# A skip term moved from VectorE into TensorE's sum over states

## The chip, the cores and the metric

The kernel runs on one NeuronCore of a Trainium2 chip. A core has engines that run beside each other, each with its own queue of instructions, which it works through in order: TensorE (PE, matrix products; its weight loads are shown apart as PEld), VectorE (DVE), ScalarE (ACT), GpSimd (POOL) and SyncE (SP, which here only issues DMAs). They wait for each other by semaphores. Data lies in SBUF (128 partitions); TensorE writes its sums to PSUM, which VectorE and ScalarE read.

The metric is the device time of one execution in microseconds (us). The profile is of one execution.

## The reference, cut to what matters

The reference runs four blocks over an image batch of 2 x 128 channels x 64 x 64: a state-space block ("the layers", two layers of Mamba with a feed-forward part), two attention blocks and a multi-scale block. The change touches the first alone. In each of its layers, with 256 inner channels and 16 states per channel:

```
u, z = split(LN(t) @ in_w.T)
u  = silu(causal_conv(u) + conv_b)
dt, B, C = split(u @ xproj_w.T);  dt = softplus(dt @ dt_w.T + dt_b)
h[t] = exp(dt * A) * h[t-1] + dt * u * B          # per channel and state
y  = sum over states of h * C  +  u * ssm_D       # the skip term is u * ssm_D
t  = t + (y * silu(z)) @ out_w.T
t  = t + ffn(LN(t))
```

`ssm_D` is one number per layer and inner channel.

## The kernel before, in words

The layers are cut into 32 items: 2 images x 2 layers x 8 chunks of 512 positions, in this order. An item has 32 slots, one for each scan. Channels and states lie together on the partitions: a group is 32 channels x 4 states (partitions) with 4 more states behind each other, so a group has four scans of 128 x 512, and an item has eight groups. The kernel's order is written out by hand: `slot` issues the recurrent work of a slot and then the entries that `background` has put at it with `at(slot, function, ...)`. Each engine works through its part of that list in order, so an entry's slot sets what it stands behind on its queue.

The recurrent work, by the names used later:

- `spread_dtu` (L406, "pdu"): TensorE spreads dt*u of a group over the states, one matmul of 128 x 128 by 512 columns, in the first slot of the group before (slots 0, 4, 8, ...). Its PSUM pool has one buffer, so it waits until `times_b` of the group before has read it.
- `times_b` (L412): VectorE multiplies it by B, into a tile `h` of 128 x 2048, in the last slot of a group (slots 3, 7, 11, ...). `h` has five buffers.
- `decay` (L419, "da"): ScalarE computes exp(dt*A) for the scan four slots later, into one of four PSUM buffers.
- `scan` (L430): VectorE's recurrence. Behind the fourth scan of a group GpSimd copies the last column (`carry`, L432) and multiplies `h` by C (L433).
- `y_pair` (L445): TensorE sums two groups over their states into one PSUM tile `py`, with 16 rows in the trace, at slots 4, 12, 20 and 28. The tile of a half (128 channels, `j` = 0 or 1) takes two `y_pair`s: slots 12 and 20 for `j` = 0, slots 28 and 4 (of the next item) for `j` = 1. `py` has one buffer.
- `y_out` (L453): VectorE computes u*ssm_D + py and writes it over u, at slot 24 for `j` = 0 and at slot 7 of the next item for `j` = 1.
- `gate` (L456): GpSimd multiplies z by it, at slot 7; `mix_out` ("po", L462) uses the product on TensorE at slot 9.

Beside this run, for the next, the same and the earlier items: convolution taps ("pu", L333, and its copy L339), "pz" (L346 and its copy L349), layer norm ("pc" L267, its square L274 and copy L275, "var" L281, the Newton step "nt" L297 on GpSimd and L298 on ScalarE, "pr" L306), silu (L353, slot 11), "pd" (L362, its copy "dbl" L366), "pt" (L381) and softplus (L387, slot 17), dt*u ("dtu", L393, GpSimd, slot 18), the feed-forward part ("ph", "hid", "pf", L478 to L499). Items 0 to 5 and 14 to 21 also do `embed` for an item two later, items 10 to 17 and from 26 on also `out_mm` for an item two earlier (L504 and L505, at slot 11).

`silu` and `soft_plus` each load a table before and after their work. All the products of layer norm, convolution, feed-forward and projections share two PSUM buffers ("mm").

Of the kernel before, what the change touches and what calls it, by code (L numbers as in the profile page):

```python
# [6 lines left out]
F32 = mybir.dt.float32  # L7
AF = mybir.ActivationFunctionType
ALU = mybir.AluOpType
# [6 lines left out]
P = 128  # L16
CH = 512
# [5 lines left out]
NJ = DI // P  # L23
# [44 lines left out]
def tile_conv_seq(ctx: ExitStack, tc, x, consts, vecs, wemb, wlay, wconv, wdt, wqkv, wsmall, wms, out):  # L68
    nc = tc.nc
# [22 lines left out]
    def load_x(b, c):  # L92
        nc.sync.dma_start(xv(b, c), x[b, :, c * RPC : (c + 1) * RPC, :])
# [6 lines left out]
    ident = kc[:, K_ID : K_ID + P]  # L100
# [3 lines left out]
    def v1(name, i=0):  # L104
        return vec[:, VEC[name] + i : VEC[name] + i + 1]
# [10 lines left out]
    with tc.manual_schedule(), ExitStack() as s:  # L116
        wp = layers.enter_context(tc.tile_pool(name="l0w", bufs=1))
        spl = layers.enter_context(tc.tile_pool(name="l0t", bufs=1))
        mm = layers.enter_context(tc.tile_pool(name="l0mm", bufs=2, space=PSUM))
        yp = layers.enter_context(tc.tile_pool(name="l0y", bufs=1, space=PSUM))  # L120
# [11 lines left out]
        sel = wp.tile([P, 32], F32, name="sel")  # L132
# [9 lines left out]

        nc.scalar.preload_act_table_set(EXP_LN_SET)
        load_x(0, 0)
        wl, wu, wd, am, cws = [], [], [], [], []

        def load_layer(l):
            cw = sp.tile([P, KC + 1, DI], F32, name="cw", tag="h", bufs=5)
# [86 lines left out]
        items = [(b, l, c) for b in range(B) for l in range(NL) for c in range(NCH)]  # L235
        NI, NST, NSL = len(items), 8, 32
        st = [{} for _ in items]
# [3 lines left out]
        def has(i):  # L241
            return 0 <= i < NI

        def vl(name, i, k=0):
            return v1(f"{name}{items[i][1]}", k)
# [189 lines left out]
        def y_pair(g):  # L435

            i, s_ = divmod(g, NST)
            j, gg = divmod(s_, 4)
            if gg == 0:
                st[i]["py", j] = yp.tile([P, CH], F32, name="py", tag="y")  # L440
            py = st[i]["py", j]
            for m in range(4):
                for k in range(2):
                    r = 32 * (gg + k)
                    nc.tensor.matmul(  # L445
                        py[r : r + 32, :], lhsT=sel, rhs=st[i]["h", s_ + k][:, m, :], start=(m == 0), stop=(m == 3),
                        tile_position=(0, r),
                    )


        def y_out(i, j):
            u = st[i]["u"][:, j, :]
            nc.vector.scalar_tensor_tensor(u, u, vl("ssm_D", i, j), st[i].pop(("py", j)), ALU.mult, ALU.add)  # L453

        def gate(i):
            nc.gpsimd.tensor_tensor(st[i]["z"], st[i]["z"], st[i]["u"], ALU.mult)  # L456
# [55 lines left out]
        def background(i):  # L512

            todo = [[] for _ in range(NSL)]

            def at(t, f, *a):
                todo[t].append((f, a))

            n, p, q, r = i + 1, i - 1, i - 2, i + 2
            if has(q):  # L520
                at(3, gelu, q)
                at(6, ffn_down, q, (0, 1)), at(7, ffn_down, q, (2, 3)), at(9, ffn_add, q)
                at(11, out_mm, q), at(12, out_add, q)
            if has(p):
                at(7, y_out, p, 1), at(7, gate, p)
                at(9, mix_out, p), at(11, mix_add, p)
            if has(n):
                at(0, pu_taps, n, 0, (0, 1)), at(1, pu_taps, n, 0, (2, 3)), at(2, pu_out, n, 0)
                at(3, pu_taps, n, 1, (0, 1)), at(4, pu_taps, n, 1, (2, 3)), at(5, pu_out, n, 1)
                at(13, xproj, n), at(14, xproj_out, n), at(14, spread_bc, n, 0), at(22, spread_bc, n, 1)  # L530
                at(15, dtproj, n, 0), at(16, dtproj, n, 1), at(17, soft_plus, n), at(18, dt_end, n)
            if has(i):
                at(1, pz_mm, i, 0), at(3, pz_out, i, 0)
                at(5, pz_mm, i, 1), at(6, pz_out, i, 1)
            if has(i) or has(n):
                at(11, silu, i, n)
            if i == -1:
                at(1, load_rest), at(7, prepare, 1), at(9, through_out)
                for k in range(3):
                    at(8 + k, fold, k), at(23, fold_out, k)  # L540
                at(19, spread_dtu, 0), at(26, times_b, 0)
            pair = [(k, second) for k, second in ((p, True), (r, False)) if has(k)]
            if has(r):
                at(10, embed, r), at(11, embed_out, r)
            w, m = {}, len(pair)
            for k, (it, second) in enumerate(pair):
                at(12 + 2 * k, ln_centre, w, k, it)
                at(13 + 2 * k, ln_square, w, k, it)
                at(27, ln_spread, w, k, m), at(28, ln_scale, w, k, it)
                at(29, ln_shift, w, k, it, second)  # L550
            if pair:
                at(17, ln_var, w, m), at(18, ln_eps, w, m), at(19, ln_rs, w, m), at(20, ln_newton, w, m), at(21, ln_step, w, m)
            if has(p):
                for f in range(4):
                    at(30 + f // 2, ffn_up, p, f)
            if has(i):
                at(24, y_out, i, 0)
            return todo
# [6 lines left out]
        def slot(i, todo, t_):  # L565
            t = i * NSL + t_
            g, m = divmod(t, 4)
            if m == 0 and 0 <= g + 3 < NG:
                spread_dt(g + 3)
            if m == 0 and 1 <= g + 1 < NG:  # L570
                spread_dtu(g + 1)
            if m == 0 and g % 2 == 1 and 0 <= g - 3 < NG:
                y_pair(g - 3)
            if 0 <= t < NT:
                scan(t)
            if 0 <= t + 4 < NT:
                decay(t + 4)
            if m == 3 and 1 <= g + 1 < NG:
                times_b(g + 1)
            for f, a in todo[t_]:  # L580
                f(*a)
        for i in range(-2, NI):
            todo = background(i)
            for t_ in range(NSL):
                slot(i, todo, t_)
        todo = background(NI)
        for t_ in range(8):
            slot(NI, todo, t_)
# [313 lines left out]
        for k in range(8, 2 * NSL):  # L902
            if k == NSL:
                todo = background(NI + 1)
            for _ in range(int(beside[k - 8]) if k - 8 < len(beside) else 0):
                next(steps, None)
            slot(NI + k // NSL, todo, k % NSL)
# [7 lines left out]
        for now in range(NALL + LAG + 8):  # L915
            r, u = divmod(now, NU)
# [65 lines left out]
    with ExitStack() as s, tc.manual_schedule():  # L982
# [59 lines left out]
        items = [(b, c) for b in range(B) for c in range(NCH)]  # L1042
        NI = len(items)
        st = [{} for _ in items]
# [433 lines left out]
```

## Time and profile before

| | |
|---|---|
| Median of 3 runs | 4975.6 us (4974.84 to 4981.31) |
| Profiled execution | 4975.69 us, span 4973.9 us |
| Layers (the part changed) | from the start to about 2102 us of the span |
| Busy over the span | PE 93%, DVE 80%, ACT 47%, POOL 47% |
| Busy in 490 to 1010 us (some eight items) | DVE 484.8, PE 474.0, ACT 381.9, POOL 371.6 of 520 us |
| VectorE's `y_out` (L453) | 64 times, 46.8 us in all, 732 ns each |
| `y_pair` on TensorE (L445) | 2048 rows, 513.6 us |

How to read it: a line of the timeline has the start in us from the start of the span, the time in us, the engine, the line of the kernel, the operation, what it writes and reads, the shapes and how many instructions are merged (x6); in brackets at the end stands how long the engine was idle before it and what ended that wait. A group has count, busy us, mean ns of one, then the idle time of the engine in front of it. A wait for several semaphores is put down to the one that came last. Matmuls are pipelined and their ends are modelled, so rows can overlap by a tenth of a microsecond or several. The granted TensorE clock is 1 at full speed.

### The profile page before, as it was taken

The numbers are of one execution on the slowest core, as the hardware profiler recorded it, in microseconds if no ns is written. First come the engines' busy times: TensorE is split into PE (matmuls) and PEld (weight loads), VectorE is DVE, ScalarE is ACT, GpSimd is POOL, SyncE is SP. The second block draws the span as 40 slices with busy tenths as digits, with TensorE's granted clock in tenths as the row PEclk, the third lists the DMA queues.
The fourth block names the chain that finished last, engine by engine and source line by source line (L and its number), as shares of the span: only waits on it lengthen the run. The fifth ranks groups of instructions, "written<-read, shape, count | busy, mean of one in ns | idle before, by whom it ended". The sixth has DMA issues, their size and how long they took to land.

```text
span 4973.9 us, 48435 instructions
## 1 busy us (share of the span) xinstructions
PE 4643.1 (93%) x14634; PEld 2218.0 (45%) x14634; DVE 3975.5 (80%) x4155; ACT 2361.8 (47%) x3225; POOL 2331.1 (47%) x1974
## 2 busy tenths in 40 slices
PE   6899999999988899899999999999999999999997
PEld 2222222222222222266667766666666666333332
DVE  6999999999999999878886677767766775667775
ACT  4677777777777777632222232233333332323332
POOL 3777776676777777613332233333333332334231
PEclk8888898988999989899999999999999999999998
DMA  6333332223333333214444444444444443000000
GB/s 163 68 67 68 69 69 67 67 67 71 69 69 69 71 73 71 69 36 126 113 111 123 113 109 115 122 99 111 114 101 98 114 112 83 3 7 7 7 5 9
DMA packets 242485, 386.28 MB, mean 78 GB/s; under 512 B 88608, under 2 KB 89136, under 8 KB 233776
## 3 DMA queue, kind: packets, MB, share of 16 engines
q1 hardware_dynamic: 193072, 316.01, 26.1%
q10 hardware_dynamic: 49152, 67.17, 5.4%
q8 instruction: 117, 1.92, 0.2%
q14 instruction: 144, 1.18, 0.1%
HBM read 101.09 MB, written 13.37 MB: 23 GB/s over the span
## 4 chain that ended last, share of the span: by engine, by line
PE 46%; POOL 25%; issue 12%; DVE 8%; DMA 4%; SPq 3%; ACT 3%; ACTq 0%; POOLq 0%; DVEq 0%
POOL h L433 19%; PE pq L780 13%; PE po L830 13%; DVE tr L810 3%; SPq L821 3%; DMA pt<-tr 3%; PE pa L677 2%; PE pf L1135 2%; PE pqkv L1162 2%; PE pw L1221 1%; POOL dtu L393 1%; POOL z L456 1%; PE pb L677 1%; PE pfus L1286 1%; PE psc L1186 1%
## 5 line engine op out<-in xcount | busy, mean ns | idle before, releaser
L817 POOL COPY pt<-tr 32x512 f32<-32x512 f32 x1024 | 644.7, 630 | 1410.8 <-DVE tr L810 700.7
L430 DVE TENSOR_TENSOR_SCAN h<-da,carry,h 128x512 f32<-128x512 f32 x1024 | 1241.6, 1265 | 65.1 <-ACT da L419 36.2
L433 POOL TENSOR_TENSOR h<-h,cb 128x2048 f32<-128x2048 f32 x256 | 1160.9, 4535 | 20.8
L780 PE MATMUL pq<-k,q 128*128 128x512 f32 x2048 | 963.4, 593 | 12.5 <-DVE sc L785 12.5
L830 PE MATMUL po<-pt,vt 128*128 128x256 f32 x4096 | 965.6, 379 | 3.5 <-POOL pt L817 3.5
L795 ACT ACTIVATE sc<-sc,nm 128x2048 f32<-128x2048 f32 x256 | 510.5, 1995 | 886.8 <-DVE nm L791 656.4
L830 PEld LDWEIGHTS po<-pt,vt 128*128 128x128 f32 x4096 | 777.9, 190 | 309.5 <-issue 227.5
L785 DVE TENSOR_SCALAR_CACHE_REDUCE sc<-pq 128x1024 f32<-128x1024 f32 x512 | 624.8, 1222 | 333.8 <-PE pq L780 311.7
L419 ACT ACTIVATE da<-dtb,am 128x512 f32<-128x512 f32 x1024 | 681.4, 684 | 221.3 <-DVE h L430 205.6
L412 DVE TENSOR_TENSOR h<-bb,pdu 128x2048 f32<-128x2048 f32 x256 | 581.4, 2271 | 85.4 <-PE py L445 28.3
L810 DVE STREAM_TRANSPOSE tr<-sc 128x2048 f32<-128x2048 f32 x256 | 591.6, 2311 | 65.7 <-DMA pt<-tr 59.3
L445 PE MATMUL py<-h,sel 128*32 128x512 f32 x2048 | 513.6, 645 | 1.8 <-POOL h L433 1.8
L780 PEld LDWEIGHTS pq<-k,q 128*128 128x128 f32 x2048 | 382.2, 190 | 291.5 <-issue 247.4
L406 PE MATMUL pdu<-dtu,fsel 128*128 128x512 f32 x512 | 327.8, 727 | 99.5 <-DVE h L412 97.5
L445 PEld LDWEIGHTS py<-h,sel 128*32 128x32 f32 x2048 | 115.6, 118 | 418.7 <-issue 413.1
L333 PE MATMUL pu<-xn,wu 128*128 128x512 f32 x512 | 245.9, 614 | 10.0 <-ACT u L339 8.3
L406 PEld LDWEIGHTS pdu<-dtu,fsel 128*128 128x128 f32 x512 | 96.6, 215 | 307.4 <-DVE h L412 180.5
L432 POOL COPY carry<-h 128x4 f32<-128x4 f32 x256 | 47.8, 187 | 390.3 <-DVE h L430 386.2
L1228 DVE TENSOR_TENSOR ov<-v,pw 128x2048 f32<-128x2048 f32 x64 | 146.2, 2284 | 65.1 <-PE pw L1221 65.1
L1162 PE MATMUL pqkv<-f,ws 128*128 128x512 f32 x384 | 188.8, 617 | 3.0 <-DVE prod L1179 2.3
L1232 POOL TENSOR_TENSOR ov<-ov 128x2048 f32<-128x2048 f32 x16 | 72.6, 4536 | 237.0 <-DVE ov L1228 237.0
L393 POOL TENSOR_TENSOR dtu<-dt,u 128x1024 f32<-128x1024 f32 x32 | 75.1, 2348 | 199.1 <-ACT dt L387 199.1
(265 smaller groups left out, 5152.4 us busy)
## 6 DMA issues: line engine op xcount, KB each, us to landing
pt<-tr SPq DMA_DIRECT2D x2048, 64.0 KB, 2.0
dtb<-dt SPq DMA_DIRECT2D x1024, 64.0 KB, 2.0
pt<-tr ACTq DMA_DIRECT2D x1024, 64.0 KB, 2.1
bb<-dr SPq DMA_DIRECT2D x128, 256.0 KB, 4.5
cb<-dr SPq DMA_DIRECT2D x128, 256.0 KB, 4.6
uw<-ufold SPq DMA_DIRECT2D x12, 576.0 KB, 4.4
uw<-dkept SPq DMA_DIRECT2D x20, 288.0 KB, 3.1
xt<-in_x SPq DMA_DIRECT2D x16, 256.0 KB, 4.8
```

The source lines that it names most:

```text
L406: nc.tensor.matmul(pdu, lhsT=four(s_ % 4), rhs=st[i]["dtu"][:, s_ // 4, :], start=True, stop=True)
L412: nc.vector.tensor_tensor(h, st[i]["bc", 0], pdu.unsqueeze(1).to_broadcast([P, 4, CH]), ALU.mult)
L419: nc.scalar.activation(da, st[i]["dtb", s_], AF.Exp, scale=am[items[i][1]][:, j, gg, m : m + 1])
L430: nc.vector.tensor_tensor_scan(h[:, m, :], da, h[:, m, :], carries[b, l][:, j, gg, m : m + 1], ALU.mult, ALU.add)
L433: nc.gpsimd.tensor_tensor(h, h, st[i]["bc", 1], ALU.mult)
L445: nc.tensor.matmul(py[r : r + 32, :], lhsT=sel, rhs=st[i]["h", s_ + k][:, m, :], start=(m == 0), stop=(m == 3), tile_position=(0, r),)
L780: nc.tensor.matmul(pq[:, i, :], lhsT=sta["q", r, grp][:, it * P : (it + 1) * P], rhs=sta["k"][:, at : at + CH], start=True, stop=True)
L785: nc.vector.tensor_scalar(dst, pq, 1.0, None, ALU.mult, ALU.max, accum_out=sta["mx"][:, c2 : c2 + 1])
L795: nc.scalar.activation(sc, sc, AF.Exp, bias=nm, scale=scale, accum_out=sm[:, hh : hh + 1])
L810: nc.vector.transpose(tr, sta.pop(("sc", r, blk, hh)).rearrange("p (t r f) -> p r t f", r=NB, f=32))
L817: nc.gpsimd.tensor_copy(dst, src)
L830: nc.tensor.matmul(sta["po", r, grp], lhsT=sta["vt"][:, jt, :], rhs=rhs, start=(jt == 0), stop=(jt == N // P - 1))
```

## The change

The term u*ssm_D is no longer added by VectorE. For each layer of each image GpSimd makes two diagonal matrices of 128 x 128 with ssm_D on the diagonal (`turn_skip`, at slot 2 of the first item of that layer, four times in all). The first `y_pair` of a half opens the sum in `py` with one matmul of the diagonal and u, 128 x 128 by 512 columns; the products over the states add to it. `y_out` becomes a copy of `py` to u on ScalarE, at the same slots as before.

```diff
             if gg == 0:
-                st[i]["py", j] = yp.tile([P, CH], F32, name="py", tag="y")
+                py = st[i]["py", j] = yp.tile([P, CH], F32, name="py", tag="y")
+                nc.tensor.matmul(py, lhsT=skip["now"][:, j, :], rhs=st[i]["u"][:, j, :], start=True, stop=False)
             py = st[i]["py", j]
             for m in range(4):
                 for k in range(2):
                     r = 32 * (gg + k)
                     nc.tensor.matmul(
-                        py[r : r + 32, :], lhsT=sel, rhs=st[i]["h", s_ + k][:, m, :], start=(m == 0), stop=(m == 3),
+                        py[r : r + 32, :], lhsT=sel, rhs=st[i]["h", s_ + k][:, m, :], start=False, stop=(m == 3),
                         tile_position=(0, r),
                     )
...
+        def turn_skip(i):
+            if items[i][2] == 0:
+                dg = skip["now"] = wp.tile([P, NJ, P], F32, name="skip", tag="skip")
+                for j in range(NJ):
+                    nc.gpsimd.tensor_tensor(dg[:, j, :], ident, vl("ssm_D", i, j).to_broadcast([P, P]), ALU.mult)
+
         def y_out(i, j):
-            u = st[i]["u"][:, j, :]
-            nc.vector.scalar_tensor_tensor(u, u, vl("ssm_D", i, j), st[i].pop(("py", j)), ALU.mult, ALU.add)
+            nc.scalar.copy(st[i]["u"][:, j, :], st[i].pop(("py", j)))
...
+            if has(i):
+                at(2, turn_skip, i)
```

More of the change, by code (lines that the diff above doesn't have):

```diff
@@ L144, in tile_conv_seq @@
         load_x(0, 0)
-        wl, wu, wd, am, cws = [], [], [], [], []
+        wl, wu, wd, am, cws, skip = [], [], [], [], [], {}
         def load_layer(l):
```

## The prediction

> **What bounds the kernel now.** The change lies in the layer stage, from the start to about 2102 us of the profiled span of 4973.9 us. I read busy time by stretches first, then the groups of instructions kept apart by shape, then the timeline of one item, engine by engine. A slot is one scan, an item is 32 slots, and a number behind a name here is the slot in its item.
>
> Busy time by stretches: length, then busy us of PE, PEld, DVE, ACT, POOL, then the granted TensorE clock.
>
> ```profile
> core 0: us, PE busy (x) PEld busy (x) DVE busy (x) ACT busy (x) POOL busy (x), PEclk, DMA share, GB/s
> 490.00:1010.00 520.00, 473.96 (x1201) 143.34 (x1199) 484.79 (x362) 381.88 (x541) 371.64 (x178) 0.89 0.32 73
> 628.70:630.70 2.00, 1.96 (x2) 0.50 (x2) 1.91 (x3) 0.59 (x1) 2.00 (x1) 0.50 0.44 101
> 635.40:662.00 26.60, 26.60 (x70) 10.13 (x68) 24.62 (x18) 18.74 (x26) 19.43 (x8) 1.00 0.14 31
> ```
>
> On average VectorE (93%) is a little fuller than TensorE (91%). The last row says more: for 26.6 us TensorE has no gap while VectorE has 2 us of them. The two take turns.
>
> Groups of the layer stage by shape (count, busy us, mean ns):
>
> ```profile
> L453 DVE SCALAR_TENSOR_TENSOR u<-u,vec,py 128x512 f32<-128x512 f32 x64 | 46.8, 732 | 8.6 <-PE py L445 8.6
> L406 PE MATMUL pdu<-dtu,fsel 128*128 128x512 f32 x512 | 327.8, 727 | 99.5 <-DVE h L412 97.5 <-POOL dtu L393 1.8
> L445 PE MATMUL py<-h,sel 128*32 128x512 f32 x2048 | 513.6, 645 | 1.8 <-POOL h L433 1.8
> ```
>
> The first is what goes. The second has the shape of the new product (128x128 weights, 512 columns; two rows for one matmul of the program).
>
> The timeline of items 8 and 9, in which the two removed VectorE instructions stand at 622.25 (slot 24 of item 8) and 653.11 (slot 7 of item 9). First VectorE; in brackets the idle time before, and what ended it:
>
> ```profile
> 622.25 0.72 DVE L453 SCALAR_TENSOR_TENSOR u<-u,vec,py 128x512 f32<-128x512 f32 x1
> 622.88 3.63 DVE L430 TENSOR_TENSOR_SCAN h<-da,carry,h 128x512 f32<-128x512 f32 x3
> ...
> 650.90 2.29 DVE L412 TENSOR_TENSOR h<-bb,pdu 128x2048 f32<-128x2048 f32 x1 [1.01 <-PE py L445]
> 653.11 0.74 DVE L453 SCALAR_TENSOR_TENSOR u<-u,vec,py 128x512 f32<-128x512 f32 x1
> ...
> 659.02 2.29 DVE L412 TENSOR_TENSOR h<-bb,pdu 128x2048 f32<-128x2048 f32 x1 [0.45 <-PE pdu L406]
> ...
> 679.85 1.28 DVE L430 TENSOR_TENSOR_SCAN h<-da,carry,h 128x512 f32<-128x512 f32 x1 [0.63 <-ACT da L419]
> ```
>
> VectorE waits for TensorE at 650.90 and 659.02, that is, on both sides of the second removed instruction. TensorE in the same time:
>
> ```profile
> 628.74 2.07 PE L406 MATMUL pdu<-dtu,fsel 128*128 128x512 f32 x2 [3.10 <-DVE h L412]
> ...
> 657.89 1.02 PE L406 MATMUL pdu<-dtu,fsel 128*128 128x512 f32 x2
> ...
> 661.36 1.12 PE L406 MATMUL pdu<-dtu,fsel 128*128 128x512 f32 x2
> 662.42 3.63 PE L445 MATMUL py<-h,sel 128*32 128x512 f32 x16
> ...
> 669.09 1.13 PE L267 MATMUL pc<-xt,kc 128*128 128x512 f32 x2
> ```
>
> At 628.74 (pdu of slot 28) TensorE has waited 3.10 us for times_b 27 on VectorE. From there to the third matmul behind 669.09 it has no idle mark. The new products stand in just this stretch: slot 28 between 628.74 and the y_pair at 630.74, slot 12 between 661.36 and 662.42. Last, ScalarE and GpSimd:
>
> ```profile
> 622.18 3.88 ACT L419 ACTIVATE da<-dtb,am 128x512 f32<-128x512 f32 x6
> ...
> 661.52 0.59 ACT L466 COPY xt<-po 128x512 f32<-128x512 f32 x1 [1.55 <-PE po L463]
> ...
> 667.98 0.57 ACT L274 ACTIVATE sq<-pc 128x512 f32<-128x512 f32 x1
> ...
> 669.55 0.58 ACT L366 COPY dbl<-pd 40x512 f32<-40x512 f32 x1
> 670.64 0.58 ACT L274 ACTIVATE sq<-pc 128x512 f32<-128x512 f32 x1
> ```
> ```profile
> 613.19 2.35 POOL L393 TENSOR_TENSOR dtu<-dt,u 128x1024 f32<-128x1024 f32 x1 [4.54 <-ACT dt L387]
> ...
> 620.25 1.26 POOL L297 TENSOR_TENSOR nt<-nt,ve 2x512 f32<-2x512 f32 x1
> ```
>
> So an item is one loop: times_b 27 releases pdu 28; TensorE runs on to po at slot 11; ScalarE waits for po, then does silu and softplus; from softplus come the decays of slots 23 and 25, for which VectorE waits; then times_b 27 again. It takes 62.36 us between the dtu of items 8 and 9, and 63.3 on average (110.08 to 2009.27 over 30 items).
>
> **What goes, part by part.** *Slot 7, VectorE.* 0.66 us from the start of the removed instruction to the next scan (653.77). The four scans are then done earlier, and times_b 11 waits for pdu 8 instead: 0.45 becomes 1.11. Bounds of the gain 0 and 0.66; I take 0, because this wait of 0.42 to 0.46 stands at the same place in 29 items (218.61 to 1992.69).
>
> *Slot 24, VectorE.* 0.63 us (622.25 to 622.88). Scan 25 also needs the first of the six decays at 622.18, six in 3.88, so it is there at 622.83. That decay is behind ScalarE's wait for nt, which comes from the softplus by dtu, h and nt on GpSimd. Gain 0.05 here. In items with more TensorE work (out_mm, items 10 to 17 and 26 on) the scan behind the removed instruction already waits (0.88 at 748.16, 0.90 at 1004.13): gain 0. Bounds 0 and 0.63; I take 0, since what is late next is shown in the row.
>
> **What comes.** *The product on TensorE.* Matmuls of that shape follow each other by 0.86 us at full clock (pdu at 657.89, po at 658.75). Where nothing is prefetched it is 1.06 (661.36 to 662.42). In slot 12 it has no wait; in slot 28 it waits for ScalarE's copy of slot 24, some 5 us earlier. I take 0.86; 1.06 is an upper end.
>
> Slot 28 is in the loop's TensorE part, with nothing to hide it: times_b 31 waits already (0.69 at 635.60; put down to a carry that ended at 635.17, but it needs the h buffer that the y_pair reads until 635.51). There the clock is 0.50, and pdu to y_pair takes 2.00 us. If the product lasts twice as long, 1.72; if full clock comes at the same moment as before (between 632.4 and 635.4), work is only moved behind that moment and the delay is 0.86. I take 0.86: with the same instructions half clock goes on for 5.3 us behind the pdu of 1010.0 in item 14, but for some 4.3 behind this one (0.89 on average from 632.4 to 635.4), so a number of matmuls does not end it. 31 of 32 items (the last has TensorE idle there, 3.26 before its ph): 31 x 0.86 = 26.7.
>
> Slot 12 splits. In items 10 to 17 and 26 to 30 TensorE limits what follows: times_b 19 waits for pdu 16 (0.48 at 799.58) or ScalarE waits for pd (0.17 at 796.34). 13 x 0.86 = 11.2; in a few of them ScalarE is the later by a few tenths, which I leave in. In the 18 items 0 to 9 and 18 to 25 ScalarE is late itself: pc of 669.09 ends at 670.22, its square starts at 670.64, so 0.42 is free, and 0.86 - 0.42 = 0.44 goes on to softplus and decay 23, where VectorE waits already (0.63 at 679.85). 18 x 0.44 = 7.9. Bounds per item 0 and 1.06.
>
> *The copies on ScalarE.* 64 of 0.59 us (the z copy of L349 has this shape: 587 ns). Behind slot 24's copy stand decays that wait for scans anyway (0.48 at 626.54, 2.87 at 630.11), so it is covered. Slot 7's copy comes behind decay 11 (654.43 to 655.1) and ends at 655.7; gate, on GpSimd, starts there instead of 654.72 and ends at 658.05, before po at 658.75. ScalarE's next wait, 1.15 for pf at 658.09, takes it up. Cost 0; without that 0.7 of cover, up to 0.6 an item, 18 in all.
>
> *The diagonals.* Four times two GpSimd products of 128x128 at slot 2. By L433 (4535 ns for 2048 columns) about 0.3 each, by L432 (187 ns for 4) at least 0.19: about 2.3 us in all, in front of GpSimd's idle time before the carry of slot 3 (1.5 to 3.7). Cost 0; at most 3. No DMA, no other queue and no table load is touched.
>
> Sum: 26.7 + 11.2 + 7.9 = 45.8. Profiled execution: 4975.69, span 4973.9 and 1.8 around it; the median of the runs is 4975.6. Forecast 4975.6 + 45.8 = 5021.
>
> **Two rules against the rows.** Row: TensorE without idle for the stretches above, VectorE waiting for it. The Trainium skill, Perfetto Trace Analysis, section Identifying the Most-Contended Engine, says that TensorE's busy share is no good measure, that its weight-load share is one, and that the engine with the highest occupancy comes first. By that TensorE stands at 28% (143.34 of 520) and VectorE at 93%, which speaks against my forecast: by the rule the sum would be 46.8 us less, about 4929. I go by the waits.
>
> The Trainium skill, TensorE: Matmul & The Clock Gate, Part 1, has the warm-up as a time of about 3.4 us in a free-running window, not a number of matmuls. By it slot 28 costs 0.86; by twice the time at half clock 1.72, 26.7 more in the sum.
>
> **Rivals.** *VectorE is the bound* (ends on the other side). For it: 93% busy, no wait from 659.02 to 679.85. Against: the waits around both removed instructions. It decides where TensorE is done before VectorE asks, that is, if the waits of 0.45 and 1.01 are not TensorE's. Price at most 64 x 0.73 = 46.8: 4929; with slot 24 alone, 32 x 0.63 = 20, 4955. Chance 0.10.
>
> *Hidden anyway.* Slot 12 covered whole, slot 24's 0.63 real: 26.7 - 20 = 7, 4982. Against: scan 25's decay. Chance 0.04 for within 0.2%, some 10 us, which is about what the measurement tells from no change.
>
> *More than the sum.* Slot 28 at 1.72 and slot 12 at 0.86 throughout: 31 x 2.58 = 80, 5056; for it the half clock at 628.70. Chance 0.16 for over 5040. That the change does not do what it says is excluded by the order of instructions: 64 products and 64 copies stand in it.
>
> **The numbers.** My forecast has 0.70, its own range 5002 (slot 12 free: 26.7) to 5041 (62 x 1.06 = 66). The range of 8 in 10 takes in most of both neighbours: 4988 to 5056. Faster 0.10, same 0.04, slower 0.86.
>
> **What would show it.** Right: times_b 11's wait for pdu grows to about 1.1 or more; the scan behind slot 24 waits for its decay, about 0.6, where it had none; items of about 64 to 66 us; VectorE's busy time down by 47, its idle time up by more. Wrong: dtu to dtu shorter than 62 us in items 2 to 9, or TensorE with idle marks between slots 28 and 12.

## The result and the profile after

The changed kernel takes 5016.99 us (median of 4 runs, 5015.78 to 5020.21), the kernel before beside it 4977.26 us (4974.84 to 4981.31). The ratio is 1.008, with a 95% interval from 1.0063 to 1.0097: slower by 31 to 48 us, where the forecast was 45.8. The profiled execution took 5016.59 us, its span 5014.8.

Of the 40.9 us between the two spans, 34.6 are there at the end of the layers: the first score product of the attention (a row of the tile pq) starts at 2229.3 instead of 2194.7. The other 6.3 come in the stages behind, which the change doesn't touch. These took between 2779.1 and 2786.2 us in the fourteen profiles of this study, one of each kernel, with the same instructions. The runs of the kernel before alone lie between 4974.8 and 4982.2 us, so with one profile each this part can't be told from scatter. Where a few microseconds matter, the layers are compared below; there too each number comes from one profile.

Busy time of the changed kernel in the stretch that was shown for before (length, then PE, PEld, DVE, ACT, POOL, granted clock):

```profile
core 0: us, PE busy (x) PEld busy (x) DVE busy (x) ACT busy (x) POOL busy (x), PEclk, DMA share, GB/s
490.00:1010.00 520.00, 469.95 (x1213) 147.71 (x1212) 468.13 (x340) 384.01 (x550) 360.56 (x172) 0.92 0.31 70
```

VectorE had 484.79 us here before and has 468.13 now. TensorE has more to do for each item and yet is not busier, since the items take longer and its clock is 0.92 instead of 0.89.

The new groups, and two that wait for the sum (count, busy us, mean ns, idle in front and its end):

```profile
L441 PE MATMUL py<-u,skip 128*128 128x512 f32 x128 | 91.5, 807 | 0.5 <-ACT u L459 0.5
L459 ACT COPY u<-py 128x512 f32<-128x512 f32 x64 | 37.2, 582 | 4.4 <-PE py L446 4.4
L462 POOL TENSOR_TENSOR z<-z,u 128x1024 f32<-128x1024 f32 x32 | 75.2, 2350 | 31.1 <-ACT u L459 31.1
L446 PE MATMUL py<-h,sel 128*32 128x512 f32 x2048 | 481.1, 612 | 3.3 <-POOL h L433 3.3
```

The gate on GpSimd now waits 31.1 us for the copy, one microsecond an item: the wait that the forecast had put under cover. The products (the first row) wait 0.5 us in all, for ScalarE's copies, so what they add to TensorE's queue is their own length and not a wait.

The timeline of items 8 and 9 of the changed kernel, VectorE first. These are the scans behind the place of the removed instruction of slot 24, then times_b 7 and times_b 11 around that of slot 7:

```profile
631.51 3.63 DVE L430 TENSOR_TENSOR_SCAN h<-da,carry,h 128x512 f32<-128x512 f32 x3 [1.57 <-ACT da L419]
...
661.22 2.29 DVE L412 TENSOR_TENSOR h<-bb,pdu 128x2048 f32<-128x2048 f32 x1 [1.01 <-PE py L446]
...
669.34 2.29 DVE L412 TENSOR_TENSOR h<-bb,pdu 128x2048 f32<-128x2048 f32 x1 [0.92 <-PE pdu L406]
```

Scan 25 waits 1.57 us for its decay where it had not waited. times_b 11 waits 0.92 for pdu 8 instead of 0.45. From times_b 7 to times_b 11 it is 8.12 us (661.22 to 669.34), and it was 8.12 before (650.90 to 659.02, in the prediction's lines): VectorE's instruction is gone from this stretch, and nothing has become shorter.

TensorE from slot 28 to slot 12 in the same items:

```profile
637.37 2.07 PE L406 MATMUL pdu<-dtu,fsel 128*128 128x512 f32 x2 [2.14 <-DVE h L412]
639.24 1.91 PE L441 MATMUL py<-u,skip 128*128 128x512 f32 x2
641.08 4.75 PE L446 MATMUL py<-h,sel 128*32 128x512 f32 x16
...
668.21 1.02 PE L406 MATMUL pdu<-dtu,fsel 128*128 128x512 f32 x2
...
671.68 1.13 PE L406 MATMUL pdu<-dtu,fsel 128*128 128x512 f32 x2
672.64 1.02 PE L441 MATMUL py<-u,skip 128*128 128x512 f32 x2
673.59 3.63 PE L446 MATMUL py<-h,sel 128*32 128x512 f32 x16
```

The products stand where they were expected, in a queue without idle marks. In slot 12 the product moves the y_pair by 0.95 us (672.64 to 673.59). In slot 28 it moves it by 1.84 (639.24 to 641.08), at half clock. From pdu 28 to pdu 8 it is 30.84 us here, and 29.15 for these items before.

### The profile page after: what moved, and what is told of

Read it like the earlier page. It is cut to its first block, busy times and chain, and to the rows that moved or that the text cites. A ratio compares the mean times of both kernels' runs of the same rounds, so it can differ in the third digit from the quotient of the medians.

```text
span 5014.8 us, 48669 instructions
## 1 busy us (share of the span) xinstructions
PE 4672.2 (93%) x14762; PEld 2247.3 (45%) x14762; DVE 3944.6 (79%) x4091; ACT 2388.8 (48%) x3289; POOL 2332.5 (47%) x1982
## 4 chain that ended last, share of the span: by engine, by line
PE 57%; DVE 12%; POOL 10%; issue 6%; DMA 6%; ACT 5%; SPq 4%; ACTq 0%; DVEq 0%; POOLq 0%
PE pq L788 12%; PE po L838 11%; POOL h L433 7%; PE py L446 5%; PE pu L333 4%; DVE tr L818 4%; DMA pt<-tr 4%; SPq L829 3%; PE pdu L406 2%; PE pa L685 2%; PE ph L484 2%; PE pf L1143 2%; ACT da L419 2%; PE pqkv L1170 2%; DVE h L412 2%
## 5 line engine op out<-in xcount | busy, mean ns | idle before, releaser
L446 PE MATMUL py<-h,sel 128*32 128x512 f32 x2048 | 481.1, 612 | 3.3 <-POOL h L433 3.3
```

The source lines that it names most:

```text
L446: nc.tensor.matmul(py[r : r + 32, :], lhsT=sel, rhs=st[i]["h", s_ + k][:, m, :], start=False, stop=(m == 3), tile_position=(0, r),)
```

## The experiments

The theory is that of the forecast: TensorE's queue from slot 28 to slot 12 sets the time of an item, the products lengthen it, and what leaves VectorE or comes to ScalarE is covered by waits. With it goes a second part, which the changed profile suggests: TensorE's granted clock, which is 0.5 or 1 and nothing else in this trace, gives some of the loss back. The rivals are that VectorE is the bound, and that ScalarE's copies (with the gate's wait) make the loss.

Four numbers are taken from the profile of each kernel. *Item* is the mean from one dtu to the next, over the 30 items from item 1 on. *Stretch* is the mean from the start of pdu 28 to the start of pdu 8 of the next item, over 29 items (from item 2's slot 28 on); slot 28's product lies in it, slot 12's behind it. *Half* is the mean time at clock 0.5 within that stretch. *At full clock* is the stretch less half of that. The kernel before, run again beside each group of these kernels, took 4976.6 to 4977.4 us, so the kernels are compared with each other directly.

| kernel | median us | ratio to before (95%) | item | stretch | half | at full clock |
|---|---|---|---|---|---|---|
| before | 4977 | 1 | 63.31 | 29.38 | 4.97 | 26.90 |
| changed | 5017.0 | 1.0080 (1.0063 to 1.0097) | 64.37 | 29.93 | 4.35 | 27.75 |
| copies on ScalarE, no product | 4981.8 | 1.0008 (0.9999 to 1.0017) | 63.27 | 29.37 | 4.95 | 26.90 |
| products, copies on VectorE | 5020.0 | 1.0086 (1.0071 to 1.0101) | 64.59 | 30.15 | 4.76 | 27.77 |
| slot 28 alone | 5009.0 | 1.0061 (1.0044 to 1.0078) | 64.23 | 30.30 | 5.04 | 27.78 |
| slot 12 alone | 4993.7 | 1.0035 (1.0022 to 1.0048) | 63.75 | 29.35 | 4.91 | 26.89 |
| each product twice | 5074.5 | 1.0192 (1.0177 to 1.0208) | 66.17 | 30.86 | 4.47 | 28.63 |
| products moved | 4971.4 | 0.9990 (0.9980 to 0.9999) | 63.07 | 29.12 | 4.29 | 26.97 |
| moved, slot 27's three times | 4957.5 | 0.9954 (0.9939 to 0.9968) | 62.48 | 27.35 | 0.13 | 27.28 |
| before, one filler | 4962.7 | 0.9970 (0.9958 to 0.9981) | 62.74 | 28.71 | 3.35 | 27.03 |
| before, two fillers | 4950.6 | 0.9947 (0.9930 to 0.9963) | 62.39 | 28.05 | 1.69 | 27.20 |
| before, three fillers | 4964.9 | 0.9974 (0.9965 to 0.9983) | 62.82 | 27.19 | 0.33 | 27.02 |
| half of the change at slot 27 | 4954.0 | 0.9952 (0.9936 to 0.9969) | 62.50 | 27.87 | 1.58 | 27.08 |
| changed, two fillers | 4993.8 | 1.0032 (1.0020 to 1.0044) | 63.73 | 28.47 | 1.18 | 27.88 |

### Copies on ScalarE, no product

```diff
-                nc.tensor.matmul(py, lhsT=skip["now"][:, j, :], rhs=st[i]["u"][:, j, :], start=True, stop=False)
...
-                        py[r : r + 32, :], lhsT=sel, rhs=st[i]["h", s_ + k][:, m, :], start=False, stop=(m == 3),
+                        py[r : r + 32, :], lhsT=sel, rhs=st[i]["h", s_ + k][:, m, :], start=(m == 0), stop=(m == 3),
```

> The copies on ScalarE stay and the skip term is left out: no product on TensorE and no instruction of VectorE for it. TensorE theory: VectorE's 46.8 us were covered by waits and the copies are covered too, so the time is that of before within 10 us (4967 to 4987). VectorE theory (it is the bound, its 47 us are worth their time): 20 to 47 us less than before (4930 to 4957). ScalarE theory (the copies and the gate's wait for them make the loss): 30 to 40 us more (5007 to 5017).

4981.79 us (ratio 1.0008, 0.9999 to 1.0017), and 63.27 us an item against 63.31. VectorE's instruction is gone, 64 copies have come to ScalarE, and the time is that of before. Both rivals fall: freeing VectorE gains nothing, and the copies cost little, 4.4 us by the medians and 1.7 at the end of the layers (2196.4). VectorE's two main groups show where the time went, in the layers before and then in this kernel:

```profile
L430 DVE TENSOR_TENSOR_SCAN h<-da,carry,h 128x512 f32<-128x512 f32 x1024 | 1241.6, 1265 | 65.1 <-ACT da L419 36.2 <-POOL carry L428 3.6 <-ACT hid L479 1.5
L412 DVE TENSOR_TENSOR h<-bb,pdu 128x2048 f32<-128x2048 f32 x256 | 581.4, 2271 | 85.4 <-PE py L445 28.3 <-PE pdu L406 22.3 <-issue 14.7
...
L430 DVE TENSOR_TENSOR_SCAN h<-da,carry,h 128x512 f32<-128x512 f32 x1024 | 1241.5, 1266 | 87.4 <-ACT da L419 54.6 <-POOL carry L428 3.6 <-ACT hid L484 1.5
L412 DVE TENSOR_TENSOR h<-bb,pdu 128x2048 f32<-128x2048 f32 x256 | 581.5, 2272 | 100.0 <-PE pdu L406 37.0 <-PE py L445 28.3 <-issue 15.5
```

The idle time has grown by 22.3 us in front of the scans (65.1 to 87.4), mostly for decays, and by 14.6 in front of times_b (85.4 to 100.0), all for pdu (22.3 to 37.0). These are the two waits that the forecast named for slot 24 and slot 7.

Since the copies came to ScalarE as VectorE's instructions went, the time alone would also fit a gain and a loss that cancel. The rows speak against it. In slot 7 the wait is for TensorE's pdu. In slot 24 of item 8 scan 25 waits for a decay that stands in front of the copy in ScalarE's queue, so the copy doesn't delay it:

```profile
623.97 3.63 DVE L430 TENSOR_TENSOR_SCAN h<-da,carry,h 128x512 f32<-128x512 f32 x3 [0.55 <-ACT da L419]
...
623.27 2.50 ACT L419 ACTIVATE da<-dtb,am 128x512 f32<-128x512 f32 x4
625.72 0.57 ACT L458 COPY u<-py 128x512 f32<-128x512 f32 x1
```

### Products, copies on VectorE

```diff
-            nc.scalar.copy(st[i]["u"][:, j, :], st[i].pop(("py", j)))
+            nc.vector.tensor_copy(st[i]["u"][:, j, :], st[i].pop(("py", j)))
```

> The products stay, the copies of the sums go back to VectorE. TensorE theory: the loss is the products', so the time is that of the changed kernel within 10 us (5007 to 5027). VectorE theory: the copies cost there what they freed, 35 to 47 us above the changed kernel (5052 to 5064). ScalarE theory: the loss goes away, about the time of before (4970 to 4990).

5020.0 us: 3 above the changed kernel. 43.2 us of work have come to VectorE (64 copies of 675 ns), and little of it is seen in the time. At the end of the layers it is 7.9 us (2237.2 against 2229.3), but the stretch at full clock is the same, 27.77 against 27.75: it holds 4.76 us at half clock instead of 4.35, and half of the 0.41, over 31 items, is 6.4. So the loss is the products'.

### Slot 28 alone, slot 12 alone

```diff
             if gg == 0:
                 py = st[i]["py", j] = yp.tile([P, CH], F32, name="py", tag="y")
-                nc.tensor.matmul(py, lhsT=skip["now"][:, j, :], rhs=st[i]["u"][:, j, :], start=True, stop=False)
+                if j == 1:        # slot 28 alone; j == 0 for slot 12 alone
+                    nc.tensor.matmul(py, lhsT=skip["now"][:, j, :], rhs=st[i]["u"][:, j, :], start=True, stop=False)
...
         def y_out(i, j):
-            nc.scalar.copy(st[i]["u"][:, j, :], st[i].pop(("py", j)))
+            if j == 1:
+                nc.scalar.copy(st[i]["u"][:, j, :], st[i].pop(("py", j)))
+                return
+            u = st[i]["u"][:, j, :]
+            nc.vector.scalar_tensor_tensor(u, u, vl("ssm_D", i, j), st[i].pop(("py", j)), ALU.mult, ALU.add)
```

> Only the second half of the channels has the change: product at slot 28, copy on ScalarE at slot 7; the first half is as before. TensorE theory: slot 28's term, 26.7 us at 0.86 each, less what a shorter time at half clock gives back: 12 to 27 us above before (4989 to 5004). VectorE and ScalarE theories see half of the copies: half of the loss, 15 to 22 us.

> Only the first half has the change: product at slot 12, copy on ScalarE at slot 24; the second half is as before. TensorE theory: slot 12's term, 19.1 us by the forecast's sum, less what the clock gives back: 5 to 19 us above before (4982 to 4996), and items 10 to 17 lose more than items 2 to 9. A theory in which nothing but the clock matters: no loss.

Slot 28 alone: 5008.95 us, 31.6 above before, a few microseconds above what was expected; at the end of the layers it is 28.2 (first score product at 2222.9 against 2194.7). The stretch is 0.92 longer and 0.88 at full clock, and the rest of the item (item less stretch) is the same, 33.93.

Slot 12 alone: 4993.68 us, 16.3 above before, and 16.0 at the end of the layers (2210.7). Here the stretch is the same, 29.35 against 29.38, and the rest of the item is 0.47 longer. Items 2 to 9 are longer by 0.32 on average (63.18 against 62.86) and items 10 to 17 by 0.62 (64.815 against 64.196), the order that was expected.

The two parts make 44.2 us in the layers when each stands alone, and 34.6 together. The 9.6 that are missing lie in the stretch: with both it is 27.75 at full clock, as with slot 28 alone (27.78), but the time at half clock is 4.35 instead of 4.97. Half of the 0.62, over 31 items, is 9.6. The two products do not bring this by themselves: with the same two and the copies on VectorE it is 4.76, and the layers take 42.5 us more than before.

### Each product twice

```diff
-                nc.tensor.matmul(py, lhsT=skip["now"][:, j, :], rhs=st[i]["u"][:, j, :], start=True, stop=False)
+                for t in range(2):
+                    nc.tensor.matmul(py, lhsT=skip["now"][:, j, :], rhs=st[i]["u"][:, j, :], start=(t == 0), stop=False)
...
                 for j in range(NJ):
                     nc.gpsimd.tensor_tensor(dg[:, j, :], ident, vl("ssm_D", i, j).to_broadcast([P, P]), ALU.mult)
+                    nc.gpsimd.tensor_tensor(dg[:, j, :], dg[:, j, :], half.to_broadcast([P, P]), ALU.mult)
```

> The changed kernel with each product split into two with half the diagonal: twice the work of TensorE in slots 12 and 28. TensorE theory: another 0.86 at slot 28 and 0.5 to 0.9 at slot 12 in each item, 35 to 55 us above the changed kernel (5052 to 5072). If the loss is not the products': within 10 us of the changed kernel.

5074.51 us, 57.5 above the changed kernel, 2 us over the upper end that was expected. In the stretch one more product is worth 0.88 at full clock again (28.63 less 27.75). The second pair of products costs more than the first, since this time the half clock gives nothing back (4.47 us against 4.35), and the slack of slot 12 is used up: the rest of the item is 35.31 against 34.44.

### Products moved into TensorE's gaps

```diff
             if gg == 0:
-                py = st[i]["py", j] = yp.tile([P, CH], F32, name="py", tag="y")
-                nc.tensor.matmul(py, lhsT=skip["now"][:, j, :], rhs=st[i]["u"][:, j, :], start=True, stop=False)
+                if j == 0:
+                    st[i]["py", j] = yp.tile([P, CH], F32, name="py", tag="y")
...
-                        py[r : r + 32, :], lhsT=sel, rhs=st[i]["h", s_ + k][:, m, :], start=False, stop=(m == 3),
+                        py[r : r + 32, :], lhsT=sel, rhs=st[i]["h", s_ + k][:, m, :], start=(j == 0 and m == 0), stop=(j == 1 and m == 3),
...
+            if gg == 2 and j == 0:
+                product(i, j, False)      # behind the y_pair of slot 20: closes the sum
...
+        def open_second(i):               # at(27, open_second, i), behind ln_spread
+            st[i]["py", 1] = yp.tile([P, CH], F32, name="py", tag="y")
+            product(i, 1, True)
```

> The change with its two products elsewhere: the first half's closes the sum behind the y_pair of slot 20 (not opens it), the second half's opens the sum at slot 27, behind the products of the layer norm. In both places TensorE has idle time before (3.10 us in front of 628.74, 1.54 in front of 623.66). TensorE theory: nearly the whole loss goes, 4965 to 4985, and half clock per item falls, since TensorE idles less. If what costs is any additional product wherever it stands: 5010 to 5020.

4971.42 us (ratio 0.9990, 0.9980 to 0.9999): the loss is gone, with the same 64 products and copies. Half clock falls from 12.88 us an item before to 9.94. TensorE around slot 27, where the timeline of before has 3.10 us without work (the third row, pdu 28):

```profile
619.58 1.98 PE L306 MATMUL pr<-rs,kc 2*128 2x512 f32 x4 [1.08 <-POOL rs L302]
621.48 1.63 PE L455 MATMUL py<-u,skip 128*128 128x512 f32 x2
624.66 2.08 PE L406 MATMUL pdu<-dtu,fsel 128*128 128x512 f32 x2 [1.54 <-DVE h L412]
```

The product fits into the gap, and 1.54 us of it are left: pdu 28 still waits for VectorE and not for the product. Part of the result is a gain by the clock: the stretch has 4.29 us at half clock instead of 4.97. But without it, too, little is lost: at full clock the stretch is 26.97 against 26.90 before, and the rest of the item 33.95 against 33.93, which makes 0.09 an item, some 3 us.

### Filling the gap, to see the clock by itself

In the first of these kernels the moved opening product is issued three times, of which the first two are overwritten:

```diff
-            product(i, 1, True)
+            for k in range(3):
+                nc.tensor.matmul(st[i]["py", 1], lhsT=skip["now"][:, 1, :], rhs=st[i]["u"][:, 1, :], start=True, stop=(k < 2))
```

> As the moved products, with the opening product of slot 27 issued three times (the first two are overwritten), so that TensorE has less idle time in front of slot 28. Clock theory: half clock per item falls by 2 to 4 us against the moved products and the time by 10 to 50 us. Queue theory: the products hold up pdu 28, and the time is 10 to 50 us above the moved ones.

4957.5 us, 14 below the moved products. Half clock per item falls by 3.2 us to 6.73, and from 4.29 to 0.13 us in the stretch. The rest of the item grows from 33.95 to 35.13, so pdu 28 is held up too, by less than the clock gains.

The others start from the kernel before and put work in the same gap that nothing uses (two, one or three products per item):

```diff
             if gg == 0:
-                st[i]["py", j] = yp.tile([P, CH], F32, name="py", tag="y")
+                if j == 0:
+                    st[i]["py", j] = yp.tile([P, CH], F32, name="py", tag="y")
...
+        def open_second(i):               # at(27, open_second, i), behind ln_spread
+            py = st[i]["py", 1] = yp.tile([P, CH], F32, name="py", tag="y")
+            for _ in range(2):
+                nc.tensor.matmul(py, lhsT=ident, rhs=st[i]["u"][:, 1, :], start=True, stop=True)
```

> The kernel before, with two products added at slot 27 of each item, whose result is overwritten: nothing else is changed. Clock theory (work in TensorE's idle time shortens the half clock and so the busy stretch behind): 10 to 50 us less than before (4927 to 4967), half clock per item down from 12.9 to 9 to 11 us. Queue theory: pdu 28 comes later by up to 1.7 us, 10 to 50 us above before. No effect: within 5 us of before.

> The kernel before with one overwritten product at slot 27. Clock theory: less filling, part of the gain: 4952 to 4972.

> The kernel before with three overwritten products at slot 27. TensorE's gap there is about 3.1 us and two products at full or half clock take 1.7 to 3.5. Clock theory: no half clock is left behind slot 28, but pdu 28 comes up to 0.9 us later: 4940 to 4970, no clear gain over two.

Two products that do nothing take 26 us off the kernel: 4950.58 (ratio 0.9947, 0.9930 to 0.9963). One takes 14 off, three 12. TensorE around slot 28 of item 8, with the y_pair of before first and then with two fillers; below it VectorE's times_b 31, before and with two; last the stretch from pdu 28 to pdu 8 with two (length, then PE, PEld, DVE, ACT, POOL, granted clock):

```profile
630.74 4.77 PE L445 MATMUL py<-h,sel 128*32 128x512 f32 x16
...
617.27 2.17 PE L306 MATMUL pr<-rs,kc 2*128 2x512 f32 x4 [0.70 <-POOL rs L302]
619.37 3.45 PE L455 MATMUL py<-u,kc 128*128 128x512 f32 x4
622.65 1.02 PE L406 MATMUL pdu<-dtu,fsel 128*128 128x512 f32 x2
623.61 3.63 PE L446 MATMUL py<-h,sel 128*32 128x512 f32 x16
627.61 3.89 PE L484 MATMUL ph<-x,wl 128*128 128x512 f32 x8 [0.37 <-ACT x L323]
```
```profile
635.60 2.29 DVE L412 TENSOR_TENSOR h<-bb,pdu 128x2048 f32<-128x2048 f32 x1 [0.69 <-POOL carry L432]
...
628.46 2.26 DVE L412 TENSOR_TENSOR h<-bb,pdu 128x2048 f32<-128x2048 f32 x1
```
```profile
622.65:650.06 27.41, 27.04 (x78) 9.54 (x77) 26.85 (x22) 19.70 (x27) 20.70 (x9) 1.00 0.15 33
```

The fillers run at half clock themselves (3.45 us for four rows). The pdu behind them runs at full clock, 1.02 instead of 2.07, and so does the y_pair, 3.63 instead of 4.77. VectorE, which waited 0.69 us at times_b 31 before, does not wait there in this item (628.46). With three fillers the stretch is shorter still, 27.19 with 0.33 us at half clock, but the rest of the item grows from 33.93 to 35.63: pdu 28 comes late. Over the 29 items it starts 0.05 us behind the end of times_b 27 before, 0.11 with one filler, 0.50 with two and 1.78 with three.

```diff
# changed kernel, with the same two overwritten products at slot 27 before the one of slot 28
+            for _ in range(2):
+                nc.tensor.matmul(py, lhsT=ident, rhs=st[i]["u"][:, 1, :], start=True, stop=True)
```

> The changed kernel with two products more at slot 27 of each item, overwritten by the one of slot 28. Clock theory: the half clock behind slot 28 goes down from 4.35 us an item to 1 to 2, TensorE's stretch from pdu 28 to pdu 8 gets 1.0 to 1.5 us shorter, and the time falls to 20 to 45 us below the changed kernel (4972 to 4997); the products of slots 12 and 28 still cost as much, so it stays 20 to 45 us above the kernel before with the same filling (4950). If filling and products don't add: outside of these.

4993.84 us: 23 below the changed kernel, and 43 above the kernel before with the same filling (4950.58). With much less half clock in the stretch of both (1.18 and 1.69 us), the products cost in all what the two parts cost alone, 43 to 44 us. It is made up otherwise, though: the stretch is 0.42 longer (0.68 at full clock), and the rest of the item 0.92, of which 0.36 is a later start of pdu 28 (0.86 us behind times_b 27 against 0.50). So the equal totals do not show that each product costs here what it costs alone.

### Half of the change, at slot 27

```diff
# second half of the channels: two products at slot 27, the first overwritten, and ScalarE's copy;
# first half: VectorE as before
+            for k in range(2):
+                nc.tensor.matmul(py, lhsT=skip["now"][:, 1, :], rhs=st[i]["u"][:, 1, :], start=True, stop=(k == 0))
```

> The second half of the channels takes the skip term from a product at slot 27, issued twice (the first is overwritten), with the copy on ScalarE; the first half stays on VectorE. TensorE theory: VectorE's instruction of slot 7 is worth nothing, so the time is that of the kernel before with two overwritten products at slot 27, 4950 within 8 us. VectorE theory: 15 to 23 us below that.

4954.01 us (0.9936 to 0.9969), as with two fillers on the kernel before. That VectorE is spared its instruction of slot 7 is worth nothing here either.

The kernel before with two fillers at slot 27 is the lowest of all: 4950.6 against 4977 and 5017. Its interval overlaps those of the mixed kernel and of the moved products issued three times, so which of the three is best stays open.

## Why the prediction was right, point by point

*The direction and its cause: right.* The products on TensorE make the loss. Without them hardly anything is lost, and with them, moved by a few slots, nothing is lost either.

*Slot 7 and slot 24 on VectorE, gain 0: right.* In slot 7 the wait for pdu 8 has taken the place; it is 0.92 and not 1.11, as the removed instruction was worth 0.47 and not 0.66. The scan now comes 2.39 us behind the start of times_b, and the removed instruction had come 2.21 behind it, so some of its 0.73 ran beside its neighbours' rows. It shows in the totals too: VectorE's busy time fell by 30.9 us (3975.5 to 3944.6), not by the 47 that was named. In slot 24 the decay holds scan 25: in item 8 by 0.55 us in the kernel with copies and no product, where about 0.6 was forecast, and by 1.57 in the changed kernel.

*Slot 28, 0.86 an item: right in size, and it was given back in part.* At equal clock the runs without fillers show 0.85 to 0.88. The price of 1.72, from the product's length at half clock, is not what it costs, though at half clock the y_pair does start 1.84 behind it. What the sum did not have is that the half clock itself gets shorter: in the changed kernel by 0.62 us an item, which makes slot 28 cost 0.55 (29.93 less 29.38). The forecast held that moment as fixed.

*Slot 12, 11.2 + 7.9 = 19.1: too large.* It measures 16.0 in the layers, 0.32 in items 2 to 9 (0.44 forecast) and 0.62 in items 10 to 17 (0.86 forecast). The few tenths of cover that the forecast saw in some of items 10 to 17 and left in would account for the second. But the half clock of an item fell as well, from 12.88 to 12.10 us, and how much of the difference is cover and how much clock stays open.

*The copies and the gate, cost 0: right.* The gate waits 31.1 us, and the kernel with copies and no product can't be told from before (0.9999 to 1.0017) and is equal in the layers within 1.7 us. The diagonals took 395 ns each on GpSimd, 3.0 us in all, and were in that kernel too.

*The sum:* 45.8 forecast, 44.2 for the two parts alone, 34.6 in the layers together, and 40.9 between the two profiles with the later stages. The step that was off is the constant clock. That the total came within 5 us is in part luck: in the layers the sum was 11.2 too high, and 6.3 of it came back in stages that the change doesn't touch.

*The two rules of the Trainium skill.* By the page Perfetto Trace Analysis, section Identifying the Most-Contended Engine, VectorE stood first, with 93% against a weight-load share of 28% for TensorE. The measurement decides against it here: 46.8 us less on VectorE gave nothing, and 43.2 us more cost 3 by the medians. Both engines are links of one loop, and a share over several items doesn't tell which link a given instruction lies in. The page TensorE: Matmul & The Clock Gate, Part 1, has the warm-up as a time and not a number of matmuls. The runs agree: with slot 28's product alone the stretch has 5.04 us at half clock against 4.97, so the added work made it hardly longer, and the price is that at full clock.

## What to carry to other kernels

Look at what the engine waits for on both sides of an instruction before counting its removal as a gain: here, in slot 7, the wait behind took its place to within a hundredth of a microsecond (8.12 us with it and without). Where work goes to an engine that is nearly full, its place in the queue decides: the same product cost about 0.9 us in front of a busy stretch and, at equal clock, less than 0.1 for both products in gaps some microseconds earlier. If TensorE's clock falls in a gap that comes back in each turn of a loop, try filling that gap with matmuls that nobody needs, as many as fit, and not more.

## What the runs showed of the hardware that was not expected

Two matmuls without use made a tuned kernel 0.5% faster (4950.6 against 4976.6 us), as the half clock went down from 12.88 to 9.03 us an item, and from 4.97 to 1.69 us in TensorE's busy stretch. With one it was 0.3%, with three 0.26%, where the stretch had almost no half clock left (0.33 us) and the queue was held up instead.

The cost of added TensorE work depends on where the clock's changes fall: the same product in slot 28 lengthened the stretch by 0.92 us alone and by 0.55 with the one of slot 12 beside it, while at full clock both are worth 0.85 to 0.88. Why the two together shorten the half clock by 0.62 us, and by 0.21 only with the copies on VectorE, was not tested by itself. That the items' length decides where the changes fall is the likely reading, and it stays a reading.
